# Two transformer layers on one core: up-projections in pairs, and another order behind the last block

## The chip, the cores and the metric

The kernel runs on one core of a Trainium2 chip. The metric is the device time of one execution in microseconds; the kernel before takes 1497.52 us, the median of 3 runs (1497.13 to 1506.65). Engines are called by the profile's names: PE is TensorE (PEld its weight loads), DVE VectorE, ACT ScalarE, POOL GpSimd, SP the engine that issues most of the DMAs.

## The reference

Four steps work one after the other on a float32 tensor of 4 x 1024 tokens of 256 elements; each one is `x = x + layernorm(f(layernorm(x)))`.

```
L0 attention: gated attention in groups of 64 tokens
   hv = silu(n @ Wh); v, gate = split(hv);  qk = silu(n @ Wqk), four scaled copies
   quad = relu(q k^T / 64 + bias)^2, causal within a group;  lin = running sum of k^T v over the groups before
   out = (gate * (quad @ v + q @ lin)) @ Wout + n
L0 feed-forward, of low rank:
   P = x @ U1            (256 -> 64)
   H = gelu(P @ V1 + b1) (64 -> 1024)
   Q = H @ U2            (1024 -> 64)
   y = Q @ V2 + b2       (64 -> 256)
L1 attention: 16 heads, relu(q k^T) divided by its row sum, projection, residual, layernorm
L1 feed-forward: 8 experts, each takes its 1024 best tokens of 4096; gelu(x W1 + b1) W2, gated, added back
```

The change bears on L0 attention and the L0 feed-forward, and on the projections for the first row of L1 attention that are made while L0 ends.

## The kernel before

The 4096 tokens are held in SBUF as eight blocks of 512 (`xs`, `NB` = 8, a block is four tiles of 128 tokens; two blocks make one of the 4 rows). The first layer is a loop over the blocks `t`. Its instructions on PE, DVE and ACT run in the very order in which the program writes them (a manual schedule); GpSimd's and SP's order is made by the framework. The program therefore weaves several streams by hand, each a list of steps with an estimated PE time:

- `main = attend(d, then)`: for each of the four tiles three steps, `out` (L822 and L826: the quadratic part and, for all but a row's first tile, the linear part; DVE then multiplies with the gate, L830), `keep` (L837: the running sum; the row's last tile issues nothing) and `finish` (L850: the output projection; DVE adds the residual, L851).
- `beside`: what is left of the feed-forward two blocks back (`left`), the projections of the coming block (`own`), and the first steps of the feed-forward of the block before (`to_hidden`: two `turn` steps, L881, which transpose the normalised tokens, and `down`, L888, whose result DVE copies to `pT`, L896).
- `hidden`: four steps `up(z)` of that feed-forward. Each makes two of the eight hidden pieces for both halves of the block's tokens. The rank is only 64, so the two halves stand in the lower and the upper 64 rows of the array. A step has four such matmuls (L906) and two gelus on ACT (L915):

```
ph = ps.tile([P, 2, 2, HB], F32, tag="g", name="ph", bufs=2)
...
nc.tensor.matmul(
    ph[:, half, k, :],
    lhsT=v1[rows, f * P : (f + 1) * P],
    rhs=d["pT"][rows, :],
    start=True,
    stop=True,
)
```

- `from_hidden`: `down2` in two halves (L927, here the two halves of the tokens stand in the left and right 64 columns of the array; DVE copies `qT`, L936) and `up2` (L946; DVE adds the bias in two instructions, L954, and starts a chain that normalises the result, statistics L560 and L561, and adds it to `xs`). These become the next block's `left`.

The loop takes one step of `main`, then, once `beside` is empty, one of `hidden`, then as many of `beside` as spread evenly. `beside` runs empty at the third `finish`, so that up-projection 0 follows the third `finish`, 1 the fourth `out`, 2 the fourth `keep` and 3 the fourth `finish`. `on_pe` also lets chains of DVE, ACT and POOL work go ahead between the steps (each `Chain` a list of small steps with a time to wait); a `turn` first finishes the chain that it reads.

Block 7 has no coming block. In its place the loop takes the projections of the first half-row (block 0) for the second layer: `turn` (L392; ACT copies to `hT`, L393), `queries` (L400; ACT splits off the high part, L408, DVE the low part, L409, SP stores both in `q_d`), `keys` (L400; L419, L420, store in `k_d`), `values` (L433; ACT copies, L441). In block 7 the feed-forward's chain also takes in the last normalisation of the attention (ACT shifts `xs` four times, L972, by `msc`, L571; DVE adds and takes statistics, L978, L560, L561; `vef`, L565, POOL's power, L567, `msf`, L571; then the rows `f`, L870).

Behind the loop a list of steps written out by hand does what remains: `left` (block 6's `down2` and `up2`), the second half-row's projections (block 1, `second[...]`), block 7's feed-forward, and the fetches `fetch_keys` (L370) and `fetch_queries` (L377) on POOL's DMA queue. Then the second layer's scores begin (L1514), with relu by ACT (L1522, L1526) and DVE (L1530).

Of the kernel before, what the change touches and what calls it, by code (L numbers as in the profile page):

```python
# [74 lines left out]
def kernel(  # L75
# [33 lines left out]
    B, S, _ = x_in.shape  # L109
# [102 lines left out]
    def act4(name):  # L212
        return acts.tile([P, NJ, D], F32, tag="act4", name=name, bufs=4)
# [8 lines left out]
    with ExitStack() as st1:  # L222
# [238 lines left out]
        def later_counts():  # L461
            r = {}

            def count_int(name, shape, pattern, per_partition, tag=None, base=0):
                n_i = const.tile(shape, I32, tag=tag or name, name=name, bufs=3 if tag else 1)
                nc.gpsimd.iota(n_i, pattern=pattern, base=base, channel_multiplier=per_partition)
                return n_i

            def count(name, shape, pattern, per_partition, dtype, base=0):
                n_i = count_int(f"{name}_i", shape, pattern, per_partition, "whole", base)  # L470
                r[name] = const.tile(shape, dtype, name=name)
                nc.gpsimd.tensor_copy(r[name], n_i)

            count("count_p", [P, P], [[1, P]], 0, BF16, 1)
            count("count_c", [P, NC], [[1, NC]], 0, BF16)
            count("count_t", [P, NTILE], [[1, NTILE]], 0, BF16)
            count("in_tile", [P, 1], [[0, 1]], 1, F32)
            r["bits0"] = count_int("bits0", [P, NVAL], [[1, NVAL]], 0)  # L480
            r["ahead_i"] = count_int("ahead_i", [P, P], [[1, P]], -1, "whole")

            quads = r["quads"] = const.tile([P, 2 * NC], F32, name="quads")
            nc.gpsimd.tensor_tensor(quads, ident[:, 0 : 2 * NC], ident[:, 32 : 32 + 2 * NC], ALU.add)
            for q in (2, 3):
                nc.gpsimd.tensor_tensor(quads, quads, ident[:, 32 * q : 32 * q + 2 * NC], ALU.add)
            return r

        def later_constants(r):
            tp = bank([P, NE * FC], "mb1_tp")  # L490
            nc.tensor.transpose(tp, mb1_rows, ident[: NE * FC, : NE * FC])
            mb1 = const.tile([P, NE * FC], F32, name="mb1")
            nc.vector.tensor_copy(mb1, tp)

            all_b = const.tile([P, P], BF16, name="all_b")
            nc.vector.memset(all_b, 1.0)
            upto_b = const.tile([P, P], BF16, name="upto_b")
            nc.vector.tensor_scalar(upto_b, r["ahead_i"], 0.0, None, ALU.is_ge)

            bits = const.tile([P, NBITS // NPER, NVAL], I32, name="bits")  # L500
            for i in range(NBITS // NPER):
                nc.vector.tensor_scalar(
                    bits[:, i, :], r["bits0"], NBITS - NPER * (i + 1), None, ALU.logical_shift_left
                )
            fold = const.tile([P, NC], BF16, name="fold")
            nc.vector.scalar_tensor_tensor(
                fold, r["quads"][:, NC : 2 * NC], float(P), r["quads"][:, 0:NC], ALU.mult, ALU.add
            )
            return mb1, all_b, upto_b, bits, fold
# [24 lines left out]
        def start(*steps):  # L534
            chains.append(Chain(steps))
            return chains[-1]

        def on_pe(us, do):
            do()
            time["now"] += us  # L540
            time["spent"] = max(time["spent"], time["now"] - 3.0)
            while time["spent"] < time["now"]:
                chain = next((c for c in chains if c.ready()), None)
                if chain is None:
                    break
                chain.go()
                time["spent"] += 1.0
# [94 lines left out]
        def residual(d):  # L642


            def apply(i0):
                if i0 == 0:
                    d["h"] = packed(d)[:, 2:4, :].rearrange("p a (b d) -> p (a b) d", d=D)
                apply_on_act(d["h"], xs[d["t"]], d["r"], i0)
                if i0:
                    nc.gpsimd.tensor_tensor(d["h"], d["h"], bo.unsqueeze(1).to_broadcast([P, NJ, D]), ALU.add)  # L650

            return [(0.0, lambda: apply(0)), (0.0, lambda: apply(2))]
# [348 lines left out]
        def woven(left, own, to_hidden):  # L1001

            return [
                *left[:2], *own[:2], *left[2:], *own[2:-2],
                *to_hidden[:1], *own[-2:-1], *to_hidden[1:2], *own[-1:], *to_hidden[2:],
            ]  # L1010

        left, ffn, take = [], ([], [], []), {}
        for t in range(NB):
            opening.finish()
            coming, after = after, None
            to_hidden, hidden, from_hidden = ffn
            adding = ahead = then = None
            if t == 0:
                whole = later_counts()
            elif t == 1:  # L1020
                mb1, all_b, upto_b, bits, fold = later_constants(whole)
                count_p, count_c, count_t, in_tile = (
                    whole[name] for name in ("count_p", "count_c", "count_t", "in_tile")
                )
            if coming is not None:
                own = project(coming)
                adding = start(*residual(coming))
            else:

                row0 = open_row(hs)  # L1030
                inputs = opening, start(*normalize_row(hs[1], 1))
                new_parts = first_parts()
                of_row = [
                    project_row(row0, k, new, inputs[k], new_parts) for k, new in enumerate((first_hT, second_hT))
                ]
                own = [
                    of_row[0][name]
                    for name in ("turn0", "turn1", "queries0", "queries1", "keys0", "keys1", "values0", "values1")
                ]
                d["y"] = wk.tile([P, NJ, D], F32, tag="nT", name="y", bufs=1)  # L1040
            if t + 2 < NB:
                after, steps = open_block(t + 2)
                opening = start(*steps)
            elif coming is not None:

                d["y"] = act4("y")
                hs = [act4("h") for _ in range(BPB)]
                opening = start(*normalize_row(hs[0], 0))
            if t >= NB - 2:
                ra, stats, scales_a, shift_a = stats_steps("c", lambda d=d: d["y"])  # L1050
                ahead, then = (ra, scales_a, shift_a), lambda i, stats=stats: stats[i][1]()
            beside = woven(left, own, to_hidden)
            main = attend(d, then)
            while main:
                on_pe(*main.pop(0))
                if not beside and hidden:
                    on_pe(*hidden.pop(0))
                places = max(len(main) - len(hidden), 0) + 1
                for _ in range(-(-len(beside) // places)):
                    on_pe(*beside.pop(0))  # L1060
            for step in (*beside, *hidden):
                on_pe(*step)
            if adding is not None:
                adding.finish()
            left = from_hidden
            ffn = feed_forward(t, lambda d=d: d["y"], ahead)
            chains.insert(0, chains.pop())
            d = coming
        to_hidden, hidden, from_hidden = ffn
        second = of_row[1]  # L1070
        take[NB - 2]()
        for step in (
            *left[:2],
            *(second[name] for name in ("turn0", "turn1")),
            *left[2:],
            second["keys0"],
            second["keys1"],
            *to_hidden[:2],
            second["values0"],
            (0.0, lambda: fetch_keys(row0, 0)),  # L1080
            (0.0, lambda: fetch_queries(row0, 0, 0)),
            *to_hidden[2:],
            *hidden,
            second["queries0"],
            *from_hidden,
            second["queries1"],
            second["values1"],
            (0.0, lambda: fetch_keys(row0, 1)),
        ):
            on_pe(*step)  # L1090
# [11 lines left out]
    with ExitStack() as st3:  # L1102
# [450 lines left out]
        beside, rest = [], []  # L1553
# [93 lines left out]
        for b in range(B):  # L1647
            after = open_row(None if b else next_hs, last=b + 2 == B) if b + 1 < B else None
            for qh in range(BPB):
# [13 lines left out]
                for q2 in range(halves):  # L1663
                    for g in range(NG):
                        for kt in range(0, KT, halves):
# [5 lines left out]
                            step = kt // halves  # L1671
# [34 lines left out]
    with ExitStack() as st4:  # L1706
# [591 lines left out]
        left = [0.0]  # L2298
# [69 lines left out]
```

## Time and profile before

| what | us |
|---|---|
| median of 3 runs | 1497.52 |
| the profiled execution | 1498.18 |
| its span, first to last instruction | 1496.4 |
| PE busy | 1443.0 |
| DVE, ACT, POOL busy | 936.5, 713.7, 518.3 |
| first layer's blocks 1 to 7, in span time | 34 to 387 |
| steps behind the last block | 387 to 420 |
| second layer's attention | 420 to 970 |

The profile is of one execution. Busy time is the time in which an engine executes; a matmul's end is modelled and lies behind the start of the next, so in lists of PE the difference of two starts is what a step takes. In such a list a line has the start in us, the time to the last end, engine, source line, operation, result and operands, shape, and the number of records (each float32 matmul gives two). In brackets stands the idle time ahead of it, with the one that ended it. The granted clock is the share of full speed that TensorE was given; over the span it was 0.985.

### The profile page before, as it was taken

What the parts mean: (1) busy time and instruction counts of PE and PEld (TensorE: products, weight loads), DVE (VectorE), ACT (ScalarE), POOL (GpSimd) and SP (SyncE); (2) the same over time, 40 slices, a digit from 0 to 9 for tenths busy, and PEclk for the clock granted to TensorE, in tenths of its full rate; (3) what the DMA queues carried; (4) which work ended last, traced back from release to release, by engine and by line L of the source; (5) the groups of instructions that cost most, each with busy time, mean ns of one, the idle gap of its engine ahead of it and who ended that gap; (6) DMA issues with size and microseconds to landing.
All of it is one profiled execution on the core that took longest, in us unless ns stands there. A gap on an engine that the chain in (4) does not pass through costs nothing. (4 is left out here: it accounts for less than half of the span.)

```text
span 1496.4 us, 24269 instructions
## 1 busy us (share of the span) xinstructions
PE 1443.0 (96%) x9240; PEld 780.3 (52%) x9240; DVE 936.5 (63%) x2221; ACT 713.7 (48%) x1182; POOL 518.3 (35%) x646
## 2 busy tenths in 40 slices
PE   8999999999899999999999999949999999999996
PEld 4666666666532333332333235517566656756764
DVE  5456655576456589659974987885545756355355
ACT  4244455444466766777676787722221232232142
POOL 4123231232250223422441323413435324553574
PEclk9999999999999999999999999979999999999998
DMA  8400000002334242533153211151424233343374
GB/s 215 139 1 1 1 1 1 1 0 82 116 99 130 69 135 64 160 99 106 61 183 114 98 52 37 44 162 37 103 29 118 46 87 59 75 100 57 64 189 114
DMA packets 91885, 121.58 MB, mean 81 GB/s; under 512 B 24925, under 2 KB 64250, under 8 KB 91642
## 3 DMA queue, kind: packets, MB, share of 16 engines
q1 hardware_dynamic: 70000, 73.09, 15.6%
q0 software_dynamic: 21712, 46.94, 13.8%
q8 instruction: 72, 1.18, 0.3%
q14 instruction: 43, 0.35, 0.1%
q10 hardware_dynamic: 58, 0.01, 0.0%
HBM read 66.90 MB, written 53.12 MB: 80 GB/s over the span
## 5 line engine op out<-in xcount | busy, mean ns | idle before, releaser
L1542 PE MATMUL po<-w,vaug 128*17 128x512 f32 (+1 forms) x2304 | 269.3, 550 | 2.8 <-DVE turned L1592 2.6
L2259 PE MATMUL py<-w,hid 128*128 128x256 f32 x1024 | 231.0, 383 | 2.1 <-ACT hid L2240 2.1
L2259 PEld LDWEIGHTS py<-w,hid 128*128 128x128 f32 x1024 | 193.3, 192 | 33.1 <-issue 4.7
L1530 DVE TENSOR_SCALAR w<-sc 128x1024 f32<-128x1024 f32 x152 | 184.8, 1221 | 35.2 <-PE sc L1514 32.8
L1522 ACT ACTIVATE w<-sc 128x512 f32<-128x512 f32 x256 | 152.9, 597 | 112.4 <-ACT w L1526 50.5
L1514 PE MATMUL sc<-q,kT 32*128 32x512 f32 (+1 forms) x2304 | 190.5, 412 | 2.2 <-ACT w L1522 1.0
L1514 PEld LDWEIGHTS sc<-q,kT 32*128 32x128 f32 x2304 | 86.2, 183 | 173.7 <-ACT w L1522 92.0
L2276 POOL DMA_INDIRECT acc_d<-y,idx x56 | 88.5, 1580 | 169.3 <-issue 37.4
L2240 ACT ACTIVATE hid<-ph,mb 128x512 f32<-128x512 f32 (+1 forms) x72 | 45.9, 638 | 160.3 <-PE ph L2233 134.5
L1526 ACT ACTIVATE w<-sc 128x512 f32<-128x512 f32 x203 | 120.2, 592 | 0.0
L2233 PE MATMUL ph<-xT,w 128*128 128x512 f32 (+1 forms) x288 | 115.3, 553 | 0.3 <-DVE xT L2124 0.3
L1528 ACT ACTIVATE w<-sc 128x1024 f32<-128x1024 f32 x104 | 106.7, 1026 | 0.0
L1948 POOL DMA_INDIRECT got<-tok_d,idx x64 | 66.1, 1033 | 75.4 <-DVE idx L1938 57.1
L1542 PEld LDWEIGHTS po<-w,vaug 128*17 128x17 f32 x2304 | 41.9, 96 | 95.3 <-issue 71.8
L2233 PEld LDWEIGHTS ph<-xT,w 128*128 128x128 f32 x288 | 52.5, 190 | 51.8 <-issue 47.7
L2274 DVE TENSOR_TENSOR y<-py,mb 128x256 f32<-128x256 f32 x56 | 23.6, 421 | 70.5 <-PE py L2259 55.8
L724 PE MATMUL pg<-nT,wh 128*128 128x512 f32 x128 | 61.6, 613 | 1.5 <-ACT nT L663 1.5
L850 PE MATMUL py<-wo,oT 128*128 128x256 f32 x256 | 61.9, 385 | 0.0
L740 PE MATMUL pv<-wh,nT 128*128 128x512 f32 x128 | 59.7, 593 | 0.0
L850 PEld LDWEIGHTS py<-wo,oT 128*128 128x128 f32 x256 | 47.3, 190 | 17.1 <-issue 9.6
L915 ACT ACTIVATE hid<-ph,vec 128x512 f32<-128x512 f32 x64 | 39.8, 685 | 27.3 <-PE ph L906 27.1
L588 POOL TENSOR_TENSOR x<-x,y 128x1024 f32<-128x1024 f32 x13 | 30.6, 2353 | 57.4 <-ACT y L577 57.4
(340 smaller groups left out, 2399.1 us busy)
## 6 DMA issues: line engine op xcount, KB each, us to landing
q<-q_d POOLq DMA_DIRECT2D x16, 1024.0 KB, 6.0
w<-in_L_ffn_W_dram SPq DMA_DIRECT2D x16, 1024.0 KB
q_d<-parts SPq DMA_DIRECT2D x48, 256.0 KB
kT<-k_d POOLq DMA_DIRECT2D x16, 512.0 KB, 4.1
k_d<-parts SPq DMA_DIRECT2D x24, 256.0 KB
acc_d<-logits SPq DMA_DIRECT2D x8, 512.0 KB
tok_d<-hg SPq DMA_DIRECT2D x30, 128.0 KB
x<-in_L_attn_x_dram SPq DMA_DIRECT2D x7, 512.0 KB
```

The source lines that it names most:

```text
L724: nc.tensor.matmul(pg, lhsT=wh[:, c, HID + e * P : HID + (e + 1) * P], rhs=d["nT"][:, c, :], start=(c == 0), stop=(c == DC - 1),)
L850: nc.tensor.matmul(py, lhsT=d["oT"][:, e, :], rhs=wo[:, e, :], start=(e == 0), stop=(e == EC - 1))
L1514: nc.tensor.matmul(sc[:, m * n : (m + 1) * n], lhsT=row["kT"][t][rows, r, (kt + m) * P : (kt + m + 1) * P], rhs=row["q"][qh, t][rows, r, p ...
L1522: nc.scalar.activation(w[:, 0, :], singles[0], AF.Relu)
L1526: nc.scalar.activation(w[:, 1, :], singles[1], AF.Relu)
L1528: nc.scalar.activation(w[:, 2:4, :], pair, AF.Relu)
L1530: nc.vector.tensor_scalar(w[:, 2:4, :], pair, 0.0, None, ALU.max)
L1542: nc.tensor.matmul(po[32 * j : 32 * j + HD + 1, weighed(halves, r)], lhsT=row["v"][:, kt + m, HQ * t + 4 * r + j, :], rhs=w[:, j, m * n : ...
L1948: return nc.gpsimd.indirect_dma_start(out=dst, out_offset=None, in_=rows[:, :], in_offset=self.at_chunk(c), bounds_check=NT - 1, oob_is_er ...
L2233: nc.tensor.matmul(ph, lhsT=w1[:, c, f * P : (f + 1) * P], rhs=xT[u][:, c, h * n : (h + 1) * n], start=(c == 0), stop=(c == DC - 1),)
L2259: nc.tensor.matmul(py, lhsT=hid[:, f, i * P : (i + 1) * P], rhs=w2[:, f, :], start=(f == 0), stop=(f == FC - 1),)
L2276: scatter = nc.gpsimd.indirect_dma_start(out=acc_d[:, :], out_offset=lists[e].at_chunk(k), in_=y, in_offset=None, bounds_check=NT - 1, oob ...
```

## The change

In the loop, an up-projection is no longer taken after each step of `main`, but two behind each other after every second one (where an even number of `main`'s steps is left). Since `beside` is empty at the third `finish`, with three steps left, the two pairs come behind the fourth `out` and behind the fourth `finish`.

In the list behind the loop, the transposes `turn0` and `turn1` of the second half-row go ahead of block 6's `down2`, and block 6's `up2` goes behind the first two steps of `to_hidden`; `values0` goes ahead of them. Block 7's up-projections are parted into two pairs with `queries0` between, and `queries1` comes ahead of block 7's `down2` and `up2`.

```diff
@@ -1053,8 +1053,9 @@
             main = attend(d, then)
             while main:
                 on_pe(*main.pop(0))
-                if not beside and hidden:
-                    on_pe(*hidden.pop(0))
+                if not beside and hidden and len(main) % 2 == 0:
+                    for step in (hidden.pop(0) for _ in range(min(2, len(hidden)))):
+                        on_pe(*step)
                 places = max(len(main) - len(hidden), 0) + 1
                 for _ in range(-(-len(beside) // places)):
                     on_pe(*beside.pop(0))
@@ -1070,20 +1071,21 @@
         second = of_row[1]
         take[NB - 2]()
         for step in (
+            *(second[name] for name in ("turn0", "turn1")),
             *left[:2],
-            *(second[name] for name in ("turn0", "turn1")),
-            *left[2:],
             second["keys0"],
             second["keys1"],
+            second["values0"],
             *to_hidden[:2],
-            second["values0"],
+            *left[2:],
             (0.0, lambda: fetch_keys(row0, 0)),
             (0.0, lambda: fetch_queries(row0, 0, 0)),
             *to_hidden[2:],
-            *hidden,
+            *hidden[:2],
             second["queries0"],
+            *hidden[2:],
+            second["queries1"],
             *from_hidden,
-            second["queries1"],
             second["values1"],
             (0.0, lambda: fetch_keys(row0, 1)),
         ):
```

## The prediction

> **What bounds the kernel now.** I read the engine lines of the page first, then stretches of the span by engine, then TensorE's own timeline inside a block and behind the last block, then VectorE's timeline there. The page:
>
> ```profile
> span 1496.4 us, 24269 instructions
> PE 1443.0 (96%) x9240; PEld 780.3 (52%) x9240; DVE 936.5 (63%) x2221; ACT 713.7 (48%) x1182; POOL 518.3 (35%) x646
> ```
>
> By stretches (columns: length, busy of PE, PEld, DVE, ACT, POOL, granted clock, DMA):
>
> ```profile
> 34.00:387.00 353.00, 352.63 (x1871) 230.73 (x1871) 202.54 (x541) 155.59 (x256) 97.59 (x71) 1.00 0.12 32
> 387.00:420.00 33.00, 26.48 (x144) 15.85 (x144) 16.60 (x48) 14.28 (x26) 9.78 (x10) 0.95 0.36 103
> ```
>
> Blocks 1 to 7 of the first layer (34 to 387) have TensorE without a gap; only what TensorE itself spends can be saved there. Behind the last block (387 to 420), 6.5 of 33 us are idle and the clock is not full: there, waits decide. TensorE in block 1 (start, time from first start to last end, line, instruction, records; a matmul has two records):
>
> ```profile
> 101.03 1.13 PE L906 MATMUL ph<-pT,v 64*128 64x256 f32 x8
> 102.10 0.49 PE L822 MATMUL po<-packed,v 128*128 128x128 f32 x2
> 102.42 0.39 PE L826 MATMUL po<-head,kv 128*128 128x128 f32 x2
> 102.65 0.39 PE L822 MATMUL po<-packed,v 128*128 128x128 f32 x2
> ...
> 103.76 0.39 PE L826 MATMUL po<-head,kv 128*128 128x128 f32 x2
> 104.08 2.00 PE L906 MATMUL ph<-pT,v 64*128 64x256 f32 x16
> 106.01 1.99 PE L850 MATMUL py<-wo,oT 128*128 128x256 f32 x8
> 107.93 1.13 PE L906 MATMUL ph<-pT,v 64*128 64x256 f32 x8
> ```
>
> Matmuls run ahead of their ends, so differences of starts count. One up-projection alone (64-row halves) takes 102.10 - 101.03 = 1.07, two behind each other 106.01 - 104.08 = 1.93: the second adds 0.86, so a group carries 0.21 of its own. The full-array step behind it takes 0.32 (102.10 to 102.42) where its like takes 0.22, and so does the one ahead (103.76 to 104.08): 0.10 each. A group costs 0.41 beyond its arithmetic. TensorE behind the last block:
>
> ```profile
> 390.16 3.70 PE L400 MATMUL pk<-hT,wk 128*128 128x512 f32 x8 [0.72 <-ACT hT L393]
> 397.08 2.21 PE L881 MATMUL tp<-ident,f 128*128 128x128 f32 x8 [3.22 <-DVE f L870]
> ...
> 403.11 2.00 PE L906 MATMUL ph<-pT,v 64*128 64x256 f32 x16 [0.53 <-DVE pT L896]
> 405.67 2.29 PE L906 MATMUL ph<-pT,v 64*128 64x256 f32 x16 [0.56 <-ACT hid L915]
> ...
> 419.73 0.92 PE L1514 MATMUL sc<-q,kT 32*128 32x512 f32 x9 [0.95 <-ACT vaug L441]
> ```
>
> **Blocks 1 to 6.** Nothing is added or removed; two up-projections now follow the fourth `out` and two the fourth `finish`. Blocks 1, 3 and 5 had three groups (the fourth `keep` issues nothing there) and get two; blocks 2, 4 and 6 had four and get two. So 3 x 1 + 3 x 2 = 9 groups fall away, on an engine with no gap: 9 x 0.41 = 3.7 us.
>
> Against this stands the Trainium skill, "TensorEngine Tiling", PSUM Bottleneck: faster tiled matmuls move the bound to those who empty PSUM. Two up-projections take 1.93 and their four gelus 2.42 (ScalarE's timeline, 105.26), and there are two banks sets `ph`. By the rule the later pair waits 0.5 in each of 7 blocks, 3.5 us. By the rows a `finish` of 1.92 lies between the pairs: gelus start 0.12 behind their group, so both sets are free 1.07 + 0.12 + 2.42 = 3.6 us after the pair began, and the fourth up-projection starts at 1.93 + 1.92 + 0.96 = 4.8. I take 0; 1.2 us are to spare. The second half of `down2`, which reads the last hidden pieces, comes 1.1 + 1.8 us behind the pair (short `out`, first half), the last gelu 1.7 behind it: also covered. ScalarE's and VectorE's order in the blocks is unchanged.
>
> **Block 7 and the steps behind it**, from the third `finish` at 373.80, the last unmoved instruction. TensorE: `finish` 1.82, fourth `out` 1.87, pair 1.93, `finish` 1.92, pair 1.93, the second half-row's transposes 1.02, `down2` 3.61: keys start at 387.9 (390.16 before). The 0.72 wait for `hT` goes, for its copies now stand ahead of the four shifts L972 on ScalarE. Keys 3.55, values 1.72: 393.2.
>
> The transposes of `f` (L881) then wait for VectorE. The copy `qT` (L936) stood ahead of L571 in VectorE's order and held the whole chain until `down2` was done (387.40); it moves behind two of four L978 steps. ScalarE: last gelu 385.0, two copies, L972 from 386.1; first L978 0.55 later, 386.65; four steps of 1.05 and L936 0.4 end at 391.2. The two adds of the second up-projection (L954, 1.25) leave the place ahead of L565; one key step L420 (0.68) comes there: L565 at 391.9. From L565 to L571 took 1.29 (GpSimd's power between), the f rows start at 393.3, and TensorE 0.55 later: 393.9. The wait is 0.7 for 3.22, with the eight transposes paced by f (1.4 for four tiles) until 395.35.
>
> What is late next: the copy `pT` (L896). VectorE before:
>
> ```profile
> 396.53 1.37 DVE L870 TENSOR_SCALAR f<-x,mvf,rsf 128x256 f32<-128x256 f32 x4
> ...
> 402.63 0.42 DVE L896 COPY pT<-pp 128x256 f32<-128x256 f32 x1 [3.12 <-PE pp L888]
> ```
>
> It stood behind three pairs of statistics that were long done. The order after has L870, the two L954, three pairs, L896; and `up2` (L946), which L954 waits for, is now between the transposes and `down`. `up2` 1.08 ends at 396.5, `down` 1.02 at 397.5; L954 396.6 to 397.85, three pairs of 0.54 minus overlap to 399.4, the copy 0.42: up-projections at 399.9. A wait of 2.35 takes the place of 0.53; queued behind L896 is one more pair and L565 `veg`, which nobody needs before 405.
>
> Then pair 1.93, queries 1.91, pair 1.93, queries 1.91, which cover the gelus (0.56 and some 0.29 of waits go, one group of 0.41 is added): 407.6. `down2` 3.61 and its 0.57 wait for `qT`: 411.75; `up2` 1.07; values and the 0.95 wait for their copy as before, 2.9: scores at 415.75, 4.0 us ahead of 419.73.
>
> Moved DMA: SP's key stores are issued 2 to 3 us earlier, and in the other order at one place (VectorE's part ahead of ScalarE's); GpSimd's key fetch behind them lands long before the scores (it was issued at 401.65). The eight query stores, at 410.52 before, begin some 6 us earlier; only the second half-row's scores read them. The first half of the fetch of the second keys still waits for `down2`; the second half is moved behind the add L588, so L588, which L954 of block 7 waits for, starts 0.73 earlier and the fetch about 2.4 later: needed 16 score steps on, some 25 us. The statistics between that L954 and the first relu L1530 gain on the scores less than TensorE does: about 0.2 lost. Tail: 3.8.
>
> **The clock.** The 4.0 contain the cold stretch behind the old wait: with clock 0.50, eight transposes took 2.00 (397.08 to 399.08) for 1.02 and values 2.42 (to 401.50) for 1.82, so 1.6. Does the new 2.35 wait bring it back?
>
> ```profile
> 396.87:400.28 3.41, 3.20 (x11) 2.69 (x12) 2.53 (x10) 1.17 (x2) 0.00 (x0) 0.50 0.51 162
> ...
> 1257.03:1260.44 3.41, 1.55 (x17) 0.40 (x16) 3.23 (x6) 0.69 (x1) 1.59 (x1) 1.00 0.59 158
> 1260.44:1263.85 3.41, 3.32 (x4) 1.18 (x4) 2.61 (x5) 1.21 (x2) 1.60 (x1) 0.50 0.14 22
> ```
>
> The Trainium skill, "TensorE: Matmul & The Clock Gate", Why this matters for your kernels, allows idle gaps up to some 3 us. By that the clock stays and the sum is 3.7 + 3.8 = 7.5. But here a stretch with 1.55 of 3.41 us busy, its gaps 1.2 and 0.8, is followed by half clock, while 31.64 to 35.05 with 1.96 busy is not. So about 1.65 idle in one stretch is enough. If the stretches' place against the program is chance, 2.35 leaves at least 1.65 in one of them with (1.06 + 1.40) / 3.41 = 0.7. I take the row: 1.6 is paid again. Sum: 7.5 - 1.6 = 5.9 us. The profiled execution had 1498.18 (span 1496.4 and 1.8 around it) and gives 1492.3; the runs' median is 0.66 lower, 1497.52, and gives 1491.6, say 1491.7.
>
> **Rivals.** (a) As above, but the wait for `pT` falls across two stretches and the clock stays: 1490.1. For it: the skill's limit; against it: the stretch at 1257. (b) Joining groups saves nothing, because each up-projection pays at its halves and not at the change to and from the full array: only the tail, -3.8 + 1.6, 1495.3. Against it: 1.93 beside 1.07. (c) Slower: ScalarE's other work gets ahead of the pairs' gelus, and TensorE waits at L906 in every block. A row scaling L577 (four, 2.07 us at 110.27) queued there would use up the 1.2 to spare; fully on the path in 7 blocks it costs 14.5: 1497.5 - 5.9 + 14.5 = 1506. It decides from 0.84 per block, gelus 2.0 later than I put them. Against it: ScalarE idles 1.4 to 1.8 ahead of the gelus in block 1, and L577 stands behind the last of them. (d) The change not doing what it says: the built order of TensorE's instructions shows the pairs, so only by (b).
>
> **Numbers.** Forecast 0.50, (a) 0.27, (b) 0.13, (c) 0.05; the rest 0.05 is more gain, where one of the other half-clock stretches (at 1260 and 1472, 1.7 each) falls away with their grid. Grid and VectorE's queue leave each case some 1.5 open: 1488.3 to 1496.2 takes in the forecast, (a) and most of (b). About 1% (15 us) is what tells a change of this kernel from none: faster by that 0.02, slower 0.04, within 0.94.
>
> **What would show it.** Right: L906 in groups of 16 records, 14 of them up to block 7, and 2.0 between their starts and the next; `keys` near 384; the wait of L881 under 1 us; a wait of L906 for `pT` L896 of about 2.3, with clock 0.50 behind it; scores near 412 in span time (3.7 from the blocks taken off my times). Wrong: waits of L906 for `hid` L915 inside the blocks, L881 still waiting over 2 us, or scores later than 417.

## The result and the profile after

The changed kernel takes 1487.93 us, the median of 8 runs (1484.52 to 1497.69); the kernel before, over all its runs beside it, 1500.87 (1497.13 to 1506.65, 8 runs). The ratio is 0.9932 with a 95% interval of 0.9905 to 0.9960: faster, by less than 1% (about 10 us; the quotient of the two medians is lower, 0.9914). The profiled execution took 1484.52, the fastest of the eight, with a span of 1482.7. The page of the changed kernel:

```profile
span 1482.7 us, 24269 instructions
PE 1435.6 (97%) x9240; PEld 778.7 (53%) x9240; DVE 937.2 (63%) x2221; ACT 712.1 (48%) x1182; POOL 518.6 (35%) x646
```

The same instructions, 7.4 us less of busy TensorE and 13.7 us less of span. By stretches (columns as before):

```profile
33.00:380.00 347.00, 346.69 (x1847) 230.89 (x1847) 203.65 (x542) 153.55 (x255) 97.54 (x71) 1.00 0.11 30
380.00:412.00 32.00, 28.03 (x172) 16.45 (x170) 16.08 (x46) 14.83 (x28) 9.35 (x10) 1.00 0.47 138
```

The blocks are still without gaps and shorter; behind them 4.0 of 32 us are idle where 6.5 of 33 were, and the granted clock is full (1.00 for 0.95). TensorE's timeline in block 1 of the changed kernel:

```profile
101.42 0.39 PE L826 MATMUL po<-head,kv 128*128 128x128 f32 x2
101.73 2.00 PE L906 MATMUL ph<-pT,v 64*128 64x256 f32 x16
103.66 1.99 PE L850 MATMUL py<-wo,oT 128*128 128x256 f32 x8
105.58 2.00 PE L906 MATMUL ph<-pT,v 64*128 64x256 f32 x16
```

Two groups of 16 records where there were one of 16 and two of 8. And behind the last block:

```profile
383.80 3.70 PE L400 MATMUL pk<-hT,wk 128*128 128x512 f32 x8
387.34 1.89 PE L433 MATMUL pv<-wv,hT 128*128 128x256 f32 x8
389.72 1.64 PE L881 MATMUL tp<-ident,f 128*128 128x128 f32 x8 [0.49 <-DVE f L870]
391.30 1.13 PE L946 MATMUL py<-v,qT 64*128 64x256 f32 x8
392.36 1.08 PE L888 MATMUL pp<-fT,u 128*64 128x256 f32 x8
395.72 2.00 PE L906 MATMUL ph<-pT,v 64*128 64x256 f32 x16 [2.27 <-DVE pT L896]
...
399.56 2.00 PE L906 MATMUL ph<-pT,v 64*128 64x256 f32 x16
...
411.33 0.97 PE L1516 MATMUL sc<-q,kT 32*128 32x512 f32 x9 [0.68 <-ACT vaug L441]
```

The wait of L881 is 0.49 for 3.22, the wait for `hT` is gone, and a wait of 2.27 for `pT` has come. VectorE in the changed kernel shows why:

```profile
389.16 1.38 DVE L870 TENSOR_SCALAR f<-x,mvf,rsf 128x256 f32<-128x256 f32 x4
392.46 1.29 DVE L954 TENSOR_TENSOR y<-py,b 128x512 f32<-128x512 f32 x2 [1.92 <-PE py L946]
...
395.27 0.39 DVE L896 COPY pT<-pp 128x256 f32<-128x256 f32 x1
```

The copy stands behind the two adds and three pairs of statistics, although `down` (L888) was done at 393.4.

To compare stages, the start-up is left out: zero is the first L724 after 30 us (34.37 before, 33.29 after; at the start the first trace has 6.8 us of half clock, the second 3.4). From zero to the first scores it was 385.36 and is 378.04: 7.3 us. From there a half-clock stretch takes 1.8 back: the first 300 records of the scores take 75.97 us for 74.13. The rest of the second layer up to the expert search is equal (409.6 from record 601 of the scores in both). The expert stage, from the first count (L1789 before, L1791 after) to the end, took 512.2 and takes 505.1. With 1.1 of start-up: 1.1 + 7.3 - 1.8 + 7.1 = 13.7.

The 7.1 us of the expert stage lie at two places where VectorE waited longer for a DMA in the trace before and TensorE stood still behind it: 1.2 us more near 1258 and 2.1 near 1470, each with a half-clock stretch after it. VectorE and then TensorE at the second place, in the kernel before:

```profile
1464.14 1.41 DVE L1989 BATCH_NORM_STATS2 stc<-back_w 128x6 f32<-128x256 f32 x4 [4.61 <-DMA back_w<-acc_d]
```

```profile
1470.23 0.70 PE L2259 MATMUL py<-w,hid 128*128 128x256 f32 x2 [1.29 <-ACT hid L2240]
1471.79 1.84 PE L2259 MATMUL py<-w,hid 128*128 128x256 f32 x4 [0.85 <-ACT hid L2240]
```

The same read-back in the changed kernel:

```profile
1450.48 1.41 DVE L1991 BATCH_NORM_STATS2 stc<-back_w 128x6 f32<-128x256 f32 x4 [0.59 <-DMA back_w<-acc_d]
```

Before, the read-back of summed rows landed late, ScalarE's scaling of them stood ahead of a gelu, and TensorE waited 2.1 us and then ran at half clock (3.4 us from 1472.07). Whether the change has a part in that is the first question to the experiments.

### The profile page after: what moved, and what is told of

It reads as the page before. It is cut to its first block, busy times and chain, and to the rows that moved or that the text cites. A ratio compares the mean times of both kernels' runs of the same rounds, so it can differ in the third digit from the quotient of the medians.

```text
span 1482.7 us, 24269 instructions
## 1 busy us (share of the span) xinstructions
PE 1435.6 (97%) x9240; PEld 778.7 (53%) x9240; DVE 937.2 (63%) x2221; ACT 712.1 (48%) x1182; POOL 518.6 (35%) x646
## 5 line engine op out<-in xcount | busy, mean ns | idle before, releaser
L724 PE MATMUL pg<-nT,wh 128*128 128x512 f32 x128 | 60.7, 606 | 1.5 <-ACT nT L663 1.5
L748 ACT ACTIVATE v<-v 128x512 f32<-128x512 f32 x32 | 20.2, 630 | 62.7 <-DVE v L747 62.7
```

## The experiments

The theory: the change moves the first layer alone, by 0.4 us for each group of up-projections that falls away and by the order of VectorE's queue behind the last block; what the expert stage adds differs from execution to execution. Rivals: the shorter first layer helps the second as well; a group costs nothing; the moved wait takes back what the list gains. All stages below are from the traces, in us: keys (L400 of the second half-row), first scores and the start of the expert search (the first count) from the zero above, the half-clock stretches of 3.4 us from 390 to 440 split into those at the list's wait and those behind the first scores, and the expert stage.

| kernel | keys | first scores | half clock: wait, scores | expert search | expert stage |
|---|---|---|---|---|---|
| before | 355.8 | 385.4 | 1, 0 | 949.8 | 512.2 |
| before, two more | 355.8, 355.8 | 386.8, 386.9 | 2, 1; 2, 1 | 952.5, 952.7 | 516.7, 505.0 |
| pairs alone, two | 352.4, 352.4 | 381.9, 383.4 | 1, 0; 2, 1 | 946.4, 949.2 | 504.7, 511.6 |
| list alone, two | 353.9, 353.9 | 383.0, 383.1 | 1, 2; 1, 1 | 950.8, 949.4 | 513.4, 505.4 |
| after | 350.5 | 378.0 | 0, 1 | 944.4 | 505.1 |
| after, once more | 350.5 | 379.6 | 1, 2 | 947.5 | 506.4 |
| down ahead of up2 | 350.5 | 375.9 | 0, 1 | 942.9 | 508.7 |
| transposes late | 352.3 | 379.7 | 0, 1 | 946.1 | 506.8 |
| function table early | 350.0 | 375.4 | 0, 1 | 942.4 | 505.0 |
| four behind each other | 367.7 | 396.6 | 1, 1 | 962.9 | 505.8 |

**The kernel before, unchanged.** No edit.

> The kernel before, unchanged. Theory (the change moves the first layer alone, the rest of the measured gain is the second layer's DMA landings of that execution): the ratio to the kernel before is 1 within its interval; in its trace the first scores start at 419.7 plus or minus 1, the expert search at 984 plus or minus 2, and the time from there to the end differs from the 512 us of the first profile by some us, with other PE waits near 1258 and 1469. Rival (the shorter first layer also helps the second): that last part is within 1 us of the first profile.

Ratio 0.9980 (0.9961 to 1.0000): no change, as it must be, and a measure of how far a ratio here can stray. The expert stage took 516.7, with a wait of 5.4 us at the place of the 1.3 and 0.9 shown above. So it varies by itself. The first scores stood at 420.7 and the search at 986.5 of the span, both just outside what was expected: two half-clock stretches more than in the first trace.

**The pairs alone.**

```diff
-                if not beside and hidden:
-                    on_pe(*hidden.pop(0))
+                if not beside and hidden and len(main) % 2 == 0:
+                    for step in (hidden.pop(0) for _ in range(min(2, len(hidden)))):
+                        on_pe(*step)
```

> Only the pairs in the loop, the list behind the loop as before. Theory: 10 groups of up-projections fewer up to block 7, 0.41 us each; the list starts 3.7 to 4.1 us earlier, the wait of L881 for f of 3.2 us and the half clock behind it stay as before (unless they fall otherwise on the grid of the clock); 3.8 us faster, ratio 0.9975. Rival (a group costs nothing, all gain is in the list): 0, ratio 1.000.

Ratio 0.9977 (0.9961 to 0.9994), some 3.4 us. The keys come 3.43 us earlier (3.7 to 4.1 expected), and the list behind them is as before, its wait for f 3.23. So a group has a price. It is not the same everywhere: taken at the start of each `down2`, the gain grows by 0.40, 0.80, 0.11, 0.80, 0.12, 0.80 and 0.40 over blocks 1 to 7. Blocks 3 and 5 should have given 0.40 each.

**The list alone.** The rest of the diff, with the loop as before.

```diff
+            *(second[name] for name in ("turn0", "turn1")),
             *left[:2],
-            *(second[name] for name in ("turn0", "turn1")),
-            *left[2:],
             second["keys0"],
             second["keys1"],
+            second["values0"],
             *to_hidden[:2],
-            second["values0"],
+            *left[2:],
...
-            *hidden,
+            *hidden[:2],
             second["queries0"],
+            *hidden[2:],
+            second["queries1"],
             *from_hidden,
-            second["queries1"],
             second["values1"],
```

> Only the other order behind the loop, the up-projections in the loop singly as before. Theory: block 7's list saves what the trace of after shows there: keys some 2 us earlier against the last finish, L881's wait 0.5 for 3.2 us, L906 waits 2.3 us for pT; from the third finish of block 7 to the first scores 3.5 to 4 us less; ratio 0.9975. Rival (the moved wait for pT takes back all): 0, ratio 1.000.

Ratio 0.9948 (0.9921 to 0.9975). First scores at 382.98: 2.4 us earlier than in the first trace of before, 3.8 and 3.9 than in the other two, which have one half-clock stretch more at the old wait. The wait for `pT` is 2.27 and brings half clock here, so that the 3.5 to 4 us expected are not reached against the first trace. The moved wait does not take back all. But behind the scores half clock costs more here, and up to the expert search the mean of the two traces is only 1.6 us ahead of the mean of the three of before; the ratio stands for 7.8 us (3.7 to 11.8). The traces of the first layer do not explain the rest.

**Down ahead of up2**, to take the wait for `pT` away.

```diff
             *to_hidden[:2],
-            *left[2:],
             (0.0, lambda: fetch_keys(row0, 0)),
             (0.0, lambda: fetch_queries(row0, 0, 0)),
             *to_hidden[2:],
+            *left[2:],
```

> The changed kernel, with block 6's up2 behind block 7's down instead of ahead of it, so that VectorE's copy pT stands ahead of the two bias adds and their statistics. Theory (the 2.3 us wait of L906 is VectorE's order alone): the wait goes, down waits some 0.4 us for fT on ScalarE in its place; first scores 1.8 to 2.0 us earlier than in the changed kernel, ratio to the kernel before about 0.0013 below that of the changed kernel in the same stage. Rival (pT waits for something else, for instance its product): L906 still waits over 1.5 us and nothing is gained.

TensorE and then VectorE with this order:

```profile
392.85 1.14 PE L888 MATMUL pp<-fT,u 128*64 128x256 f32 x8 [0.29 <-ACT fT L882]
393.92 1.13 PE L946 MATMUL py<-v,qT 64*128 64x256 f32 x8
394.89 1.89 PE L906 MATMUL ph<-pT,v 64*128 64x256 f32 x16
...
414.24 1.22 PE L1516 MATMUL sc<-q,kT 32*128 32x512 f32 x6 [0.67 <-DVE w L1532]
```

```profile
394.04 0.42 DVE L896 COPY pT<-pp 128x256 f32<-128x256 f32 x1 [2.30 <-PE pp L888]
395.08 1.29 DVE L954 TENSOR_TENSOR y<-py,b 128x512 f32<-128x512 f32 x2 [0.62 <-PE py L946]
```

The copy runs as soon as its product is there, beside `up2`, and L906 waits for nothing; 0.29 for `fT` is what it costs. First scores 2.14 us earlier than in the changed kernel (1.8 to 2.0 expected). The wait was VectorE's order alone. Of the 2.14, 0.7 is lost again at the scores, which now wait 0.67 for the first relu on VectorE (last line of the first list): 300 records on, this order is 1.45 ahead. Ratio 0.9908 (0.9880 to 0.9935).

**The changed kernel once more.** No edit.

> The changed kernel, unchanged. Theory (the change moves the first layer alone): from the first projection after 30 us to the first scores 378.0 us as in its first profile, on 0.1 us; half-clock stretches near the pT wait and the first scores come and go with the clock's grid (up to 3.4 us); the second layer's expert stage takes other times (505 us in the first profile, 512 to 517 before); ratio to the kernel before 0.9945 to 0.996. Rival (the change also shortens the second layer): expert stage again 505 plus or minus 2 and ratio 0.991 to 0.993.

Ratio 0.9944 (0.9922 to 0.9966). Here the wait for `pT` brings half clock, and the first scores are at 379.6, 1.6 later. The expert stage took 506.4, as the rival would have it; the ratio lies at the edge of the theory's 0.9945 to 0.996, and its interval takes in the rival's 0.993 too. This run does not decide between them.

**The function table early**, on top of down ahead of up2.

```diff
                 if z == 0:
                     d["hid"] = [act8("hid", "hid") for _ in range(2)]
+                    nc.scalar.activation(warm, mhalf[:, 0:1], AF.Gelu_apprx_tanh)
```

> As the run with down first, and a gelu of one element is issued on ScalarE ahead of each block's first up-projection, so that the function table is loaded before the product is there. Theory (the late gelus of blocks 3 and 5, which keep the fourth up-projection 0.29 us, come from the table load of 1.28 us behind the wait): first gelus of blocks 2 to 6 start 1.28 us earlier, both waits go, first scores 0.6 us earlier than with down first alone, 375.3 us after the first projection. Rival (four gelus of 0.6 us are too slow for a pair of up-projections anyway): no change, 375.9.

In block 3 of the changed kernel, TensorE's last pair and then ScalarE:

```profile
198.34 2.28 PE L906 MATMUL ph<-pT,v 64*128 64x256 f32 x16
```

```profile
195.72 1.28 ACT L915 ACT_TABLE_LOAD   x1 [4.49 <-PE ph L906]
197.01 2.42 ACT L915 ACTIVATE hid<-ph,vec 128x512 f32<-128x512 f32 x4
199.59 2.42 ACT L915 ACTIVATE hid<-ph,vec 128x512 f32<-128x512 f32 x4 [0.15 <-PE ph L906]
```

With the table asked for early:

```profile
199.31 2.00 PE L907 MATMUL ph<-pT,v 64*128 64x256 f32 x16
```

```profile
192.21 1.28 ACT L901 ACT_TABLE_LOAD   x1
193.50 0.20 ACT L901 ACTIVATE warm<-mhalf 128x1 f32<-128x1 f32 x1
196.69 2.42 ACT L916 ACTIVATE hid<-ph,vec 128x512 f32<-128x512 f32 x4 [2.99 <-PE ph L907]
```

ScalarE goes from silu to gelu, and the table load of 1.28 us starts only when the first product is there. The first gelus end 1.28 late, and the fourth up-projection, which needs their bank, takes 0.29 more (2.28 for 2.00). With the load ahead, blocks 3 and 5 gain their 0.40 as well: keys at 349.96 for 350.50, first scores at 375.38 (375.3 expected). This is the fastest first layer of all, 10 us ahead of the first trace of before (7.4 at the expert search); ratio 0.9935 (0.9910 to 0.9959), which the other stages' spread does not set apart from the changed kernel's.

**Four behind each other**, one group a block.

```diff
-                if not beside and hidden and len(main) % 2 == 0:
-                    for step in (hidden.pop(0) for _ in range(min(2, len(hidden)))):
-                        on_pe(*step)
+                if not main:
+                    while hidden:
+                        on_pe(*hidden.pop(0))
```

> The changed kernel with all four up-projections behind the fourth finish, so one group a block. Theory (a group costs 0.40, but without a finish between them TensorE waits for the gelus of two sets of banks): 7 groups fewer save 2.8 us, 1.1 us of wait per block as behind the last block before the change, and up to 1.3 more in blocks 2 to 6 where the table load lies behind the first product: the steps of block 7's down2 start 5 to 11 us later than in the changed kernel. Rival (gelus keep up): 2.8 us earlier.

TensorE and ScalarE in block 2 of this kernel:

```profile
153.27 2.00 PE L906 MATMUL ph<-pT,v 64*128 64x256 f32 x16
157.11 2.80 PE L906 MATMUL ph<-pT,v 64*128 64x256 f32 x16 [1.84 <-ACT hid L915]
```

```profile
154.50 1.28 ACT L915 ACT_TABLE_LOAD   x1 [7.26 <-PE ph L906]
155.79 3.83 ACT L915 ACTIVATE hid<-ph,vec 128x512 f32<-128x512 f32 x6
```

Keys 17.2 us later than in the changed kernel, 5 to 11 expected: waits of 1.84 ahead of the second pair and 0.29 within it in blocks 2 to 6, of 0.50 and 0.29 in blocks 1 and 7, and in blocks 1, 3, 5 and 7 another 0.78 of the fourth `finish` for `oT`, which the pair between had covered and which the expectation missed. In block 2 the wait also brings a half-clock stretch (from 158.75, behind one with 1.62 of 3.41 us busy), which costs 1.6 us; the 2.80 above is a pair partly at half clock. And one group fewer gains nothing here: block 4 loses 2.2 us, all of its waits. The one execution took 1505.92. What hides the gelus is the `finish` between the pairs; with it out of the way, the rule on emptying PSUM that the prediction weighed shows in these waits.

**The transposes late.**

```diff
-            *(second[name] for name in ("turn0", "turn1")),
             *left[:2],
+            *(second[name] for name in ("turn0", "turn1")),
             second["keys0"],
```

> The changed kernel with the second half-row's transposes behind block 6's down2 again, so that VectorE's copy qT stands ahead of the shift factors L571. Theory (that place of the copy held the chain): L571 waits for down2 again, the four shifts L972 and the copies of hT come some 1.5 us later; keys wait 1.7 to 2 us for hT, first scores 1.4 us later than in the changed kernel. Rival (the wait for f went because up2's bias adds left the place ahead of it): first scores within 0.3 us of the changed kernel.

TensorE with this order:

```profile
387.05 3.70 PE L400 MATMUL pk<-hT,wk 128*128 128x512 f32 x8 [1.78 <-ACT hT L393]
...
392.83 1.64 PE L881 MATMUL tp<-ident,f 128*128 128x128 f32 x8 [0.36 <-DVE f L870]
```

The wait stands ahead of the keys instead, 1.78, and first scores come 1.7 us later than in the changed kernel (1.4 expected). So moving the transposes, and with them `qT` in VectorE's order, is worth 1.7 of the list's gain.

**Three traces more**, because the ten so far had a long expert stage in just the three kernels without pairs.

> The kernel before once more, for its trace. In the ten traces so far the expert stage takes 512 to 517 us in the three without pairs in the loop and 504.7 to 508.7 in the seven with them. Theory (its DMA landings differ from execution to execution, whatever the first layer does): any value from 504 to 517 here. Rival (the pairs shorten it): 512 or more.

> Only the pairs in the loop, once more. Theory (landings by execution): expert stage anywhere from 504 to 517 us. Rival (the pairs shorten it): below 509. By both, the start of block 7's down2 is 372.0 us after the first projection when one half-clock stretch lies ahead of it, and the half clock behind the first scores comes only if the grid of the clock puts a stretch from about their start to 3 or 4 us later.

> Only the other order behind the loop, once more. Theory (landings by execution): expert stage anywhere from 504 to 517 us. Rival (without the pairs it is long): 512 or more. First scores 381.4 us after the first projection if the wait for pT brings no half clock, 383.0 if it does.

505.0 and 505.4 without pairs, 511.6 with them: the expert stage reaches from 505 to 517 us in the kernel before alone, and the rival that the pairs shorten it falls. That the change as a whole makes the long ones rarer is not ruled out: the six traces of the changed kernel and its variants have 505.0 to 508.7, and of the other seven four have over 511. First scores of the list alone at 383.06, with half clock at the wait for `pT`:

```profile
397.70:401.11 3.41, 1.14 (x11) 0.61 (x8) 3.27 (x11) 0.00 (x0) 0.75 (x1) 1.00 0.75 223
401.11:404.52 3.41, 3.41 (x16) 2.27 (x14) 0.18 (x2) 1.80 (x3) 1.03 (x1) 0.50 0.15 47
```

## Why the prediction was right, and where it was not

It said 1491.7, 1488.3 to 1496.2, within 1%. The measured median, 1487.93, lies 0.4 below that range, the ratio of 0.9932 is under the forecast's 0.9961, and the repeat's interval (0.9922 to 0.9966) holds it. The direction and the steps hold; sizes were off. Up to the expert search, half clock included, the forecast's 5.9 us were 5.4 between the two first profiles and 5.7 between the means of three traces before and two after. That the sum fits so well is in part luck: the blocks gave less than said, the list more, and two terms of the clock that were left out pull against each other. What the ratio has beyond that comes behind it.

**Groups in the blocks.** The price of 0.41 is right, 0.40 measured. The sum of 3.7 for blocks 1 to 6 was 3.03, and the part that failed is "gelus start 0.12 behind their group ... I take 0". Block 1, from which the 0.12 was read, has its table load ahead; in blocks 2 to 6 it lies behind the first product, so that the 1.2 us to spare were not there. The trace of before had it, in block 3:

```profile
196.21 1.28 ACT L915 ACT_TABLE_LOAD   x1 [2.70 <-PE ph L906]
```

In blocks 2, 4 and 6 the `keep` covers the late gelus, in 3 and 5 0.29 comes through: 0.6 us, between the 0 of the rows and the 3.5 of the rule on PSUM. That is rival (c) in small, by the table load and not by the row scaling that it named.

**The list.** Keys were put at 387.9 less 3.7, 349.8 from the zero; measured 350.5, and 0.6 of the 0.7 are blocks 3 and 5. L881's wait: 0.7 said, 0.49 measured. The wait for `pT`: 2.35 said, 2.27 measured, for the reason given. First scores: 377.7 said, 378.0 measured, a gain of 7.7 said and 7.3 measured. Of that the blocks gave 0.7 less than said and block 7 with the list 0.3 more. (The sum of 7.5 took off 0.2 more for VectorE behind the first scores, which no run here isolates.)

**The clock.** The forecast paid 1.6 again behind the wait for `pT`, with a chance of 0.7; of the six traces with that wait, four show half clock behind it and two, the profiled one among them, do not. In the four, 2.1 to 2.3 us of the wait lie in one stretch, in the two at most 1.2 and 1.5; the forecast's limit of about 1.65 lies between. The profiled execution is thus rival (a):

```profile
391.26:394.67 3.41, 2.18 (x17) 1.18 (x16) 2.14 (x6) 0.83 (x2) 0.75 (x1) 1.00 0.57 187
394.67:398.08 3.41, 2.36 (x17) 1.76 (x18) 1.65 (x7) 1.12 (x2) 1.03 (x1) 1.00 0.54 152
...
411.74:415.15 3.41, 2.68 (x24) 1.08 (x16) 3.07 (x10) 2.27 (x5) 1.84 (x2) 1.00 0.87 274
415.15:418.56 3.41, 3.41 (x22) 0.81 (x24) 3.12 (x7) 1.24 (x3) 3.41 (x4) 0.50 0.34 114
```

The wait falls across the border of two stretches and leaves each over 2.1 us of work. The limit of some 3 us that the Trainium skill gives for an idle gap ("TensorE: Matmul & The Clock Gate", Why this matters for your kernels) would have kept the clock in all six; the measured rows decide against it.

Two terms of the clock were missing. Behind the first scores 11 of 13 traces lose a stretch or two, and the first profile is one of the two that don't: 1.8 us here, as the last two lines show. And the old wait costs one stretch in the profile that the sum was made on, but two in three of the five traces that have it (scores at 386.8 for 385.4). The first takes from the gain that one profile showed, the second adds to it. The first comes in all eight traces with the new list and in three of the five with the old; whether the new list makes it likelier, so few traces do not show.

**What the range left out.** The expert stage differs by up to 12 us between executions. The two profiles that are compared had 512.2 and 505.1; the kernel before alone reaches from 505.0 to 516.7, so no step of the change is needed for that. But the ratio stands for 10 us (6 to 14), the repeat's for 8.4 (5 to 12), and the traces show 5.7 up to the search. Whether the remainder is chance, or the change, its list above all, makes a long expert stage rarer, stays open. Rival (b) fell with the pairs alone.

## What to carry to other kernels

Matmuls that use half of the rows of the array were worth putting side by side here, 0.40 us for each group that fell away, but count the work that fills the time while their banks are emptied, and look for a table load that waits with the first of their activations. When a step is moved, follow every instruction that its product sets off through the queue of its engine: here two adds and three statistics went ahead of a copy that TensorE waited for, and one line in the list takes 2.1 us of that back at the first scores. Before a profile's difference is explained, run the old kernel again and compare stage by stage: the keys repeat to 0.02 us, the first scores to 0.1 where the half-clock stretches are as many, the last stage not to 10.

## What was not expected of the hardware

Half clock does not follow from busy time alone. In the changed kernel a stretch with 2.68 of 3.41 us busy, nearly all of it the first scores (32 of 128 rows to a matmul) with small waits, is followed by a clock of 0.50, while stretches with 2.18 and 2.36 busy of larger matmuls are not. Nor is one with 2.79 busy of the same scores in the kernel before:

```profile
420.76:424.17 3.41, 2.79 (x27) 1.08 (x31) 3.34 (x7) 3.01 (x6) 3.30 (x4) 1.00 0.54 199
424.17:427.58 3.41, 3.41 (x36) 0.95 (x36) 3.27 (x8) 2.17 (x4) 3.33 (x3) 1.00 0.44 171
```

The half clock begins 2.6 to 3.9 us after the first score in all 11 traces that have it. What the clock counts, these runs don't show. And the table load of 1.28 us that was put ahead of a gelu began, in blocks 2 to 6, only when the gelu's own input had arrived, though ScalarE had been idle for 4.49 us; in block 1 it ran ahead of that input (at 98.48 in the changed kernel, the gelus at 102.91). Why the two differ is open.
